# Linear-attention layer of a four-layer trunk: value projection in two parts, later affine on ScalarE, longer rows of convolution matrices

## The chip, the cores and the metric

The kernel runs on one core of a Trainium2 chip, in float32. The metric is the device time of one execution in microseconds (us), as the median of several runs.

## The reference

The input x is [1, 512, 64, 64]. Four layers follow each other, each of the form `x = x + layer(groupnorm(x))`: an attention with distances (layer 0), two gated convolution layers (1 and 2), and the linear attention with a depthwise 5x5 convolution that is changed here (layer 3). Cut to what matters:

```python
def _L3_conv_ref(x, ...):                       # D = 256, EPS = 1e-5
    qkv0 = affine(conv1x1(x, w_qkv), s_qkv, b_qkv)            # 768 channels
    agg = affine(depthwise5x5(qkv0, w_dw), s_dw, b_dw)
    agg = agg * (w_pw * s_pw) + b_pw
    q, k, v = split(concat([qkv0, agg], axis=1), 3)           # 512 channels each
    q = relu(q) + EPS
    k = relu(k) + EPS
    z = einsum('bc,bcn->bn', k.mean(axis=2), q) + EPS
    vk = einsum('bcn,bdn->bcd', v * N ** -0.5, k * N ** -0.5)
    attn = einsum('bcd,bdn->bcn', vk, q) / z
    y = attn * g_norm + bt_norm + v
    return affine(conv1x1(y, w_proj), s_proj, b_proj)

x = x + L0(gn(x));  x = x + L1(gn(x));  x = x + L2(gn(x));  x = x + L3(gn(x))
```

In chunks of 128 channels, qkv0 has chunks 0 to 5 and agg chunks 0 to 5. So q is qkv0[0..3], k is qkv0[4..5] with agg[0..1], and v is agg[2..5]. The projection of v, `w_proj v`, does not depend on the attention and can be added to x by itself.

## The kernel before

The state X, 512 channels by 4096 pixels, stays in SBUF as four chunks of 128 partitions through all layers. Pixels are held as 4 x 8 planes (by the pixel's row and column modulo), and a block is 512 pixels. In layer 3 a block has the indices `hf` (0 or 1, half of the image) and `q` (0 to 3).

**Instruction order.** The program is written with a framework that plans the order: on each engine a planner places instructions by their written order and by when its cost model believes them ready, and it adds the semaphore waits. Only TensorE keeps the written order (`keep_in_program_order`, L684 and L1335). Each engine then executes its list in order; DMAs are issued from the lists of SyncE (SP), ScalarE and POOL, so an issue that waits holds up what stands behind it there.

**Layer 3, making qkv0.** `fused` and `group` make qkv0 (with products saved by sums and differences, `_Seven`), and `put` writes each result through a plane tile to a DRAM buffer G (L711). The pieces are kept in the list `made`, 81 of them, and `fill(n)` executes the next n. The weights come from `weights` (L1112), which loads a chunk and multiplies it on POOL by a broadcast row of `s_qkv`; `scales` (L1122) loads that row into buffers of the pool `kv`, in two loads on ScalarE's queue.

**The depthwise convolution.** `_PlaneConv.conv` handles chunk i, half hf as block-structured matrix products. `load` (L716) brings two rounds at once: the matrices T (one DMA, L720) and two copies of the input S (two DMAs, L737), of which ScalarE (L744) or VectorE (L742) makes the shifted second copies. A convolution is two halves of 64 products (128 matmul instructions each). After each half VectorE transposes the two PSUM banks into `turned` (L798), after the second it makes four blocks `agg` (L807), and the callback `finish` is called for each: in layer 3 `affine` (L1291), an activation on ScalarE. `conv` yields after the first half and at its end. `ahead` issues the loads of the next convolution early; `sp3` has four buffers each of T and S.

**`convs(units, between)`** (L1299) runs convolutions one after the other, and at each yield it takes one function of `between`, TensorE work that goes between two halves. In the list of before, the order is (0,0), (1,0) with four fills, then (2,0), (0,1), (3,0), (4,0), (5,0) with four fills for the first four yields and then `added` (a bias row, 16 tiny products), `prepare(0,0)` (loads and sums k) and three `turned` (transposes of k, L1345).

**The steps.** For each of the eight blocks, `step(t)` (L1359), four times, transposes k and v (L1336, evicted as kT on ScalarE and vT on VectorE), projects v for output chunk t (`part`, L1348: four products with `w_proj`, an eviction `pv` on ScalarE, an addition to X on POOL, L1355), and accumulates the four v-k products in the banks `vkp`. The steps of hf=0 run among the convolutions (1,1) to (5,1), the steps of hf=1 after them. All products, convolution halves and transposes share four PSUM banks, `ps_mm`. Then q is loaded, and the output is made block by block.

Of the kernel before, what the change touches and what calls it, by code (L numbers as in the profile page):

```python
# [25 lines left out]
D = C // HEADS  # L26
GROUP = 16
GN_EPS = 1e-5


KS = 7
# [93 lines left out]
@with_exitstack  # L125
def trunk_kernel(ctx: ExitStack, tc: tile.TileContext, a: dict, out: bass.AP):
    nc = tc.nc

    base = ctx.enter_context(tc.tile_pool(name="base", bufs=1))
    small = ctx.enter_context(tc.tile_pool(name="small", bufs=1))  # L130


    X = base.tile([P, NC, N], FP, tag="X", name="X")
    for b in range(NB):
        for c in range(NC):
            eng = nc.sync if c % 2 == 0 else nc.scalar
# [28 lines left out]

    neg2 = base.tile([D, 1], FP, tag="neg2", name="neg2")
    nc.vector.memset(neg2, -2.0)

    def new_stats():
        return small.tile([P, NC, NB, 6], FP, tag="stats", name="stats")  # L170

    centered = _Centered(tc, small)

    dram = ctx.enter_context(tc.tile_pool(name="dram", bufs=1, space=bass.MemoryType.DRAM))
    F = [dram.tile([P, FORM.planes, FORM.plane], FP, tag=f"F{i}", name=f"F{i}") for i in range(NDW)]
    F3 = [
        dram.tile([P, FORM3.planes, FORM3.plane], FP, tag=f"G{i}", name=f"G{i}")
        for i in range(NQKV)
    ]
    Z = dram.tile([NB, BLK], FP, tag="Z", name="Z")  # L180

    stats = _attention(tc, a, X, ident, gmask, neg2, small, new_stats, centered)
    stats = _gated_convs(tc, a, X, vcol, gmask, small, new_stats, centered, stats, F)
    _linear_attention(tc, a, X, vcol, vall, ident, gmask, small, centered, stats, F3, Z, out)


def _attention_general(tc, a, X, O, ident, neg2):
# [469 lines left out]
class _PlaneConv:  # L657
# [58 lines left out]
    def load(self, i, hf, wT, r):  # L716
        nc, f = self.nc, self.f
        nl = self.nl
        w = self.sp3.tile([P, nl, 4, f.by * f.bx, 32], FP, tag="T", name="T")
        nc.sync.dma_start(  # L720
            out=w.rearrange("p r g b m -> p r (g b m)"),
            in_=wT[i, r : r + nl].rearrange("r p x -> p r x"),
        )
        run = (f.part + f.by - 1 + (f.jy - 1) * f.by) * f.fw
        S = self.sp3.tile([P, nl, 4, run], FP, tag="S", name="S")
        F = self.F[i]
        chan = f.planes * f.plane
# [174 lines left out]
def _gated_convs(ctx, tc, a, X, vcol, gmask, small, new_stats, centered, stats, F):  # L902
# [7 lines left out]
    hp = ctx.enter_context(tc.tile_pool(name="ch", bufs=5))  # L910
    ps_mm = ctx.enter_context(tc.tile_pool(name="ps_mm", bufs=4, space=PSUM))
    ps_cv = ctx.enter_context(tc.tile_pool(name="ps_cv", bufs=4, space=PSUM))
    pc = _PlaneConv(ctx, tc, FORM, F, ps_cv, 2, 4, False)

    for layer in ("L1", "L2"):
        pre = f"{layer}_conv_"
# [133 lines left out]


@with_exitstack
def _linear_attention(ctx, tc, a, X, vcol, vall, ident, gmask, small, centered, stats, F, Z, out):

# [48 lines left out]
    with ExitStack() as st:  # L1103
        wp = st.enter_context(tc.tile_pool(name="lw", bufs=1))
        w2p = st.enter_context(tc.tile_pool(name="lw2", bufs=4))
        tmp = st.enter_context(tc.tile_pool(name="ltmp", bufs=5))
        kvp = st.enter_context(tc.tile_pool(name="kv", bufs=34))
        ps_vk = st.enter_context(tc.tile_pool(name="ps_vk", bufs=1, space=PSUM))
        ps_mm = st.enter_context(tc.tile_pool(name="ps_mm", bufs=4, space=PSUM))
        pc = _PlaneConv(st, tc, f, F, ps_mm, 2, 4, True)  # L1110

        def weights(i, scale):  # L1112
            t = w2p.tile([P, NROW], FP, tag="w", name="w_qkv")[:, 0:C].rearrange(
                "p (c n) -> p c n", c=NC
            )
            nc.sync.dma_start(out=t, in_=a["L3_w_qkv"][i])
            nc.gpsimd.tensor_tensor(
                t, t, scale.unsqueeze(1).to_broadcast([P, NC, P]), ALU.mult
            )
            return t  # L1120

        def scales(i, n):  # L1122

            t = kvp.tile([P, BLK], FP, tag="kv", name="s_qkv")[:, 0 : n * P]
            nc.scalar.dma_start(
                out=t, in_=bass.AP(a["L3_s"].tensor, a["L3_s"].offset + i * P, [[0, P], [1, n * P]])
            )
            return t.rearrange("p (i m) -> p i m", m=P)

        s_qkv = scales(0, 4)  # L1130
        w_qkv = [weights(i, s_qkv[:, i]) for i in range(4)]

        alpha = wp.tile([P, NQKV], FP, tag="alpha", name="alpha")
        beta = wp.tile([P, NQKV], FP, tag="beta", name="beta")
# [120 lines left out]
            return [lambda: taken(2 * k), lambda: taken(2 * k + 1)]  # L1255

        def more_weights():
            s4 = scales(4, 2)
            for i in (4, 5):
                w_qkv.append(centered.scaled(weights(i, s4[:, i - 4]), rstd, nc.scalar))  # L1260

        dve, pool = nc.vector, nc.gpsimd
        made = [
# [24 lines left out]
        def conv(i, hf, primed):  # L1288
            agg[i, hf] = [kvp.tile([P, BLK], FP, tag="kv", name=f"agg{i}") for _ in range(4)]

            def affine(t):  # L1291
                nc.scalar.activation(  # L1292
                    t, t, AF.Relu if i < 2 else AF.Identity,
                    bias=beta[:, i : i + 1], scale=alpha[:, i : i + 1],
                )

            return pc.conv(i, hf, a["L3_T"], affine, agg[i, hf], primed)

        def convs(units, between, before=0):  # L1299


            between = list(between)
            if before:
                pc.ahead(*units[0], a["L3_T"])
                for _ in range(before):
                    between.pop(0)()
            for n, u in enumerate(units):
                for part, _ in enumerate(conv(*u, n + before > 0)):
                    if between:
                        between.pop(0)()  # L1310
                    if part == 0 and n + 1 < len(units):
                        pc.ahead(*units[n + 1], a["L3_T"])
            for f in between:
                f()

        agg = {}
        def gather(hf, q):
# [27 lines left out]
            def turned(t):  # L1345
                ahead[t] = turn(ks, t, "kT", kvp, "kv")

            def part(o, v):  # L1348
                ps = product(lambda c: w_proj[:, c, ts(o, P)], v)
                t = tmp.tile([P, BLK], FP, tag="tmp", name="pv")  # L1350
                nc.scalar.activation(
                    t, ps, AF.Identity, bias=pbias[:, o : o + 1], scale=vcol(pre + "s_proj", o)
                )
                xs = blocks(X[:, o, :])[:, hf, q]
                nc.gpsimd.tensor_tensor(  # L1355
                    xs, xs, t.rearrange("p (x n) -> p x n", x=XW), ALU.add
                )

            def step(t):  # L1359
                v = [agg[2 + i, hf][q] for i in range(NC)]  # L1360
                kT = ahead.pop(t) if t in ahead else turn(ks, t, "kT")
                vT = turn(v, t, "vT")
                part(t, v)
                for c in range(NC):
                    pc.matmul(
                        vkp[c],
# [3 lines left out]
                        stop=(b == NB - 1 and t == QT - 1),  # L1370
                    )

            return prepare, turned, [lambda t=t: step(t) for t in range(QT)]

        def both(*pieces):
            return lambda: [f() for f in pieces]
# [26 lines left out]
        def prepare(hf, q):  # L1403
            return blks[hf, q][0]
# [4 lines left out]
        def steps(hf, q):  # L1409
            return list(blks[hf, q][2])  # L1410

        convs(
            [(2, 0), (0, 1), (3, 0), (4, 0), (5, 0)],
            fills(6, 6, 6, 6)
            + [added, prepare(0, 0), turned(0, 0, 0), turned(0, 0, 1), turned(0, 0, 2)],
        )
        vkp = [ps_vk.tile([P, C], FP, tag=f"vk{c}", name=f"vkp{c}") for c in range(NC)]
        for q in range(3):
# [196 lines left out]
```

## Time and profile before

| | |
|---|---|
| time, median of 3 runs | 3947.94 us (3947.69 to 3948.85) |
| the profiled execution's own time | 3946.93 us |
| its span, from first to last instruction | 3945.0 us |
| TensorE (PE) busy | 3856.6 us, 98% |
| VectorE (DVE) busy | 2363.8 us, 60% |
| ScalarE (ACT) busy | 1968.2 us, 50% |
| POOL busy | 96.2 us, 2% |
| mean granted TensorE clock | 0.991 |
| T loads: layers 1 and 2 / layer 3 | 112 x 384 KB / 48 x 256 KB |

Busy shares are means over four quite different layers. The granted clock is the share of full speed at which TensorE was allowed to run; a product at half clock counts as busy for twice the time. The last layer begins at about 3306 us, and the steps of hf=1 end at about 3808 us. In the profile's lines an arrow reads "written from read"; in brackets stands the idle time before, and what ended it.

### The profile page before, as it was taken

How to read it: one execution, taken by the hardware profiler on the slowest of the kernel's cores; microseconds unless marked ns; L12 is line 12 of the kernel's file. 1: busy time of each engine (PE TensorE's matmuls, PEld its weight loads, DVE VectorE, ACT ScalarE, POOL GpSimd, SP SyncE). 2: the span in 40 equal slices, each digit the busy share in tenths (PEclk: the TensorE clock that was granted, in tenths of full speed). 3: DMA queues.
4: the chain of work that ended last, by engine and by line, in shares of the span. 5: the costliest groups of instructions: out<-in, count | busy, mean ns of one | idle time of the engine just before them, and what ended most of it. 6: DMA issues, size and time to landing. Idle time of an engine off the chain costs nothing. (4 is left out here: it accounts for less than half of the span.)

```text
span 3945.0 us, 81422 instructions
## 1 busy us (share of the span) xinstructions
PE 3856.6 (98%) x35622; PEld 1721.0 (44%) x35622; DVE 2363.8 (60%) x2607; ACT 1968.2 (50%) x2841; POOL 96.2 (2%) x84
## 2 busy tenths in 40 slices
PE   6999999999999999999999989999999998989999
PEld 4533345333354333453333345554455543455544
DVE  3677763777737777547767633466434567664435
ACT  3577753777726777446656544451344522343210
POOL 0000000000000000000000000000000000201110
PEclk9999999999999999999999999999999999989999
DMA  2000000000000000000000045651255521563334
GB/s 97 9 1 1 1 1 9 1 1 1 1 1 9 1 1 1 1 9 1 1 1 1 1 130 154 186 154 57 69 161 177 162 56 51 153 171 85 92 90 142
DMA packets 214631, 221.52 MB, mean 56 GB/s; under 512 B 13416, under 2 KB 179688, under 8 KB 214144
## 3 DMA queue, kind: packets, MB, share of 16 engines
q1 hardware_dynamic: 187312, 157.12, 14.6%
q10 hardware_dynamic: 26928, 59.11, 4.1%
q8 instruction: 281, 4.60, 0.5%
q14 instruction: 78, 0.64, 0.1%
q0 software_dynamic: 32, 0.06, 0.0%
HBM read 156.46 MB, written 59.77 MB: 55 GB/s over the span
## 5 line engine op out<-in xcount | busy, mean ns | idle before, releaser
L507 ACT ACTIVATE pt<-ps_s,A 128x512 f32<-128x512 f32 x2048 | 1286.3, 687 | 554.8 <-PE ps_s L499 527.0
L590 DVE TENSOR_TENSOR acc<-acc,pt 128x1024 f32<-128x1024 f32 x960 | 1175.4, 1224 | 331.8 <-ACT pt L507 306.0
L517 PE MATMUL av<-pt,V 64*64 64x512 f32 x8192 | 1112.5, 590 | 0.9 <-ACT pt L507 0.9
L499 PE MATMUL ps_s<-O,K 64*64 64x512 f32 x8192 | 1111.5, 589 | 0.0
L517 PEld LDWEIGHTS av<-pt,V 64*64 64x64 f32 x8192 | 339.7, 133 | 557.2 <-issue 525.4
L499 PEld LDWEIGHTS ps_s<-O,K 64*64 64x64 f32 x8192 | 334.3, 133 | 553.7 <-issue 308.6
L744 ACT COPY S<-S 32x1295 f32<-32x1295 f32 (+1 forms) x272 | 341.0, 1256 | 300.6 <-DMA S<-F 203.4
L684 PE MATMUL ps<-X,w_in_L 128*128 128x512 f32 x896 | 405.9, 605 | 5.4 <-DVE w_in_L L357 5.4
L957 DVE TENSOR_SCALAR plane<-ps,vec 128x512 f32<-128x512 f32 x112 | 83.8, 748 | 295.3 <-PE ps L684 252.3
L684 PEld LDWEIGHTS ps<-X,w_in_L 128*128 128x128 f32 x896 | 167.0, 192 | 205.1 <-issue 195.4
L684 PE MATMUL ps_cv<-S,T 64*32 64x128 f32 x13824 | 240.5, 278 | 13.3 <-issue 5.5
L684 PEld LDWEIGHTS ps_cv<-S,T 64*32 64x32 f32 x13824 | 199.1, 107 | 117.7 <-issue 81.6
L454 PE MATMUL ps_qk<-X,wqkv 128*128 128x512 f32 x512 | 227.2, 597 | 2.8 <-ACT wqkv L354 2.8
L684 PE MATMUL ps<-h,w_out_L 128*128 128x512 f32 x512 | 228.4, 599 | 0.5 <-DVE X L991 0.5
L346 ACT ACTIVATE X<-X,gn_less 128x512 f32<-128x512 f32 x120 | 77.1, 710 | 217.5 <-DVE gn_less L100 206.4
L458 ACT ACTIVATE O<-ps_qk 128x512 f32<-128x512 f32 x32 | 19.1, 596 | 258.3 <-PE ps_qk L454 258.3
L1016 ACT ACTIVATE h<-h,vec 128x1024 f32<-128x1024 f32 x56 | 63.7, 1148 | 167.3 <-DVE h L804 167.1
L684 PEld LDWEIGHTS ps<-h,w_out_L 128*128 128x128 f32 x512 | 94.3, 190 | 116.6 <-issue 100.5
L454 PEld LDWEIGHTS ps_qk<-X,wqkv 128*128 128x128 f32 x512 | 95.5, 192 | 113.5 <-issue 109.9
L979 DVE SCALAR_TENSOR_TENSOR h<-ps,vec,h 128x512 f32<-128x512 f32 x112 | 82.5, 743 | 103.1 <-PE ps L684 99.0
L684 PE MATMUL ps<-h,pw_L 128*128 128x512 f32 x320 | 142.6, 598 | 0.7 <-DVE X L995 0.7
L460 DVE TENSOR_SCALAR K<-ps_qk 128x512 f32<-128x512 f32 x32 | 22.1, 692 | 187.0 <-PE ps_qk L454 187.0
(153 smaller groups left out, 2745.5 us busy)
## 6 DMA issues: line engine op xcount, KB each, us to landing
T<-in_L_T_dram SPq DMA_DIRECT2D x112, 384.0 KB, 4.0
F<-plane ACTq DMA_DIRECT2D x112, 324.0 KB, 2.7
S<-F SPq DMA_DIRECT2D x224, 162.0 KB, 4.1
row<-G SPq DMA_DIRECT2D x80, 272.0 KB, 3.7
S<-G SPq DMA_DIRECT2D x96, 153.0 KB, 4.5
G<-plane ACTq DMA_DIRECT2D x48, 289.0 KB, 2.3
T<-in_L_T_dram SPq DMA_DIRECT2D x48, 256.0 KB, 4.1
out_dram<-y SPq DMA_DIRECT2D x32, 256.0 KB, 2.0
```

The source lines that it names most:

```text
L346: self.nc.scalar.activation(xs, xs, AF.Identity, bias=less)
L454: nc.tensor.matmul(ps, w[:, n, c, :], X[:, c, cols], start=(c == 0), stop=(c == NC - 1))
L460: nc.vector.tensor_scalar(K[:, cols], ps, gain_in, None, ALU.mult)
L499: nc.tensor.matmul(ps[ts(half, D), ts(h, BLK)], K[rows, t * P + half * D : t * P + (half + 1) * D], QO[pair][rows, cols], start=True, stop ...
L507: nc.scalar.activation(pt[:, ts(h, BLK)], ps[:, ts(h, BLK)], AF.Exp, bias=A[:, t, h : h + 1])
L517: nc.tensor.matmul(av[half][rows, :], V[keys, t, rows], pt[keys, ts(h, BLK)], start=(t == 0), stop=(t == NT - 1),)
L590: nc.vector.tensor_add(acc, acc, pt)
L684: self.tc.keep_in_program_order(self.nc.tensor.matmul(*args, **kw))
L744: nc.scalar.copy(second, first)
L957: lambda dst, src: nc.vector.tensor_scalar(dst, src, vcol(pre + "b_in", 1 + i), None, ALU.add),
L979: nc.vector.scalar_tensor_tensor(d, ps, bias, d, ALU.add, ALU.mult)
L1016: nc.scalar.activation(t, t, AF.Identity, bias=vcol(pre + "dw_b", i))
```

## The change

Five edits, four of them in layer 3.

1. `part(o, c0, c1)` projects only the chunks c0 to c1 of v. For the blocks of hf=0 the chunks 0 and 1 (agg[2], agg[3]) are projected in 16 early parts, each with its own eviction (without bias) and its own addition to X; the steps of hf=0 project chunks 2 and 3. The steps of hf=1 project all four as before.
2. The convolutions are run in another order: (2,0), (3,0) with the four fills, then (0,1), (4,0), (5,0) with `added`, the 16 early parts (1, 3, 3, 3, 3, 3) and `prepare(0,0)` between their halves. The three early `turned` of block (0,0) are gone; its steps do those transposes. (0,1) is now the first of its list, so its loads are written at its start and not in the previous convolution.
3. `affine` is put into a list `late`, and run after the next piece of `between`.
4. `s_qkv` is loaded once, from POOL's queue before layers 1 and 2, into a pool of its own; the pool `kv` has 33 buffers in place of 34.
5. The matrices T are laid out in DRAM so that the two rounds of a load are contiguous for each partition: one row of twice the length per partition. This holds for layers 1 to 3.

```diff
+    late = ctx.enter_context(tc.tile_pool(name="late", bufs=1))
+    s_qkv = late.tile([P, NQKV, P], FP, tag="s_qkv", name="s_qkv")
+    nc.gpsimd.dma_start(
+        out=s_qkv.rearrange("p i m -> p (i m)"),
+        in_=bass.AP(a["L3_s"].tensor, a["L3_s"].offset, [[0, P], [1, NQKV * P]]),
+    )
     stats = _gated_convs(tc, a, X, vcol, gmask, small, new_stats, centered, stats, F)
...
         nc.sync.dma_start(
-            out=w.rearrange("p r g b m -> p r (g b m)"),
-            in_=wT[i, r : r + nl].rearrange("r p x -> p r x"),
+            out=w.rearrange("p r g b m -> p (r g b m)"), in_=wT[i, r // nl],
         )
...
-        kvp = st.enter_context(tc.tile_pool(name="kv", bufs=34))
+        kvp = st.enter_context(tc.tile_pool(name="kv", bufs=33))
...
-        s_qkv = scales(0, 4)
-        w_qkv = [weights(i, s_qkv[:, i]) for i in range(4)]
+        w_qkv = [weights(i) for i in range(4)]
...
             def affine(t):
-                nc.scalar.activation(
-                    t, t, AF.Relu if i < 2 else AF.Identity,
-                    bias=beta[:, i : i + 1], scale=alpha[:, i : i + 1],
+                late.append(
+                    lambda: nc.scalar.activation(
+                        t, t, AF.Relu if i < 2 else AF.Identity,
+                        bias=beta[:, i : i + 1], scale=alpha[:, i : i + 1],
+                    )
                 )
...
                     if between:
                         between.pop(0)()
+                    while late:
+                        late.pop(0)()
                     if part == 0 and n + 1 < len(units):
                         pc.ahead(*units[n + 1], a["L3_T"])
...
-            def part(o, v):
-                ps = product(lambda c: w_proj[:, c, ts(o, P)], v)
+            def part(o, c0, c1):
+
+                ps = product(
+                    lambda c: w_proj[:, c0 + c, ts(o, P)],
+                    [agg[2 + c, hf][q] for c in range(c0, c1)],
+                )
                 t = tmp.tile([P, BLK], FP, tag="tmp", name="pv")
-                nc.scalar.activation(
-                    t, ps, AF.Identity, bias=pbias[:, o : o + 1], scale=vcol(pre + "s_proj", o)
-                )
+                scale = vcol(pre + "s_proj", o)
+                if c1 == NC:
+                    nc.scalar.activation(t, ps, AF.Identity, bias=pbias[:, o : o + 1], scale=scale)
+                else:
+                    nc.scalar.activation(t, ps, AF.Copy, scale=scale)
...
-                part(t, v)
+                part(t, 0 if hf else 2, NC)
...
+            early = [lambda o=o: part(o, 0, 2) for o in range(NC)]
+            return prepare, turned, [lambda t=t: step(t) for t in range(QT)], early
...
+        convs([(2, 0), (3, 0)], fills(6, 6, 6, 6))
+
+        early = [f for q in range(4) for f in blks[0, q][3]]
         convs(
-            [(2, 0), (0, 1), (3, 0), (4, 0), (5, 0)],
-            fills(6, 6, 6, 6)
-            + [added, prepare(0, 0), turned(0, 0, 0), turned(0, 0, 1), turned(0, 0, 2)],
+            [(0, 1), (4, 0), (5, 0)],
+            [
+                both(added, *early[:1]),
+                both(*early[1:4]),
+                both(*early[4:7]),
+                both(*early[7:10], prepare(0, 0)),
+                both(*early[10:13]),
+                both(*early[13:]),
+            ],
         )
...
-        return T.reshape(n // P, f.nr, P, -1)
+        T = T.reshape(n // P, f.nr // NL, NL, P, -1)
+        return T.swapaxes(2, 3).reshape(n // P, f.nr // NL, P, -1)
```

More of the change, by code (lines that the diff above doesn't have):

```diff
@@ L28 @@
 GN_EPS = 1e-5
+NL = 2
 KS = 7
@@ L182, in trunk_kernel @@
     stats = _attention(tc, a, X, ident, gmask, neg2, small, new_stats, centered)
+    late = ctx.enter_context(tc.tile_pool(name="late", bufs=1))
[4 more added lines that the diff above has]
+    )
     stats = _gated_convs(tc, a, X, vcol, gmask, small, new_stats, centered, stats, F)
-    _linear_attention(tc, a, X, vcol, vall, ident, gmask, small, centered, stats, F3, Z, out)
+    _linear_attention(tc, a, X, vcol, vall, ident, gmask, small, centered, stats, F3, Z, s_qkv, out)
 def _attention_general(tc, a, X, O, ident, neg2):
@@ L912, in _gated_convs @@
     ps_cv = ctx.enter_context(tc.tile_pool(name="ps_cv", bufs=4, space=PSUM))
-    pc = _PlaneConv(ctx, tc, FORM, F, ps_cv, 2, 4, False)
+    pc = _PlaneConv(ctx, tc, FORM, F, ps_cv, NL, 4, False)
     for layer in ("L1", "L2"):
@@ L1052, in _linear_attention @@
 @with_exitstack
-def _linear_attention(ctx, tc, a, X, vcol, vall, ident, gmask, small, centered, stats, F, Z, out):
+def _linear_attention(ctx, tc, a, X, vcol, vall, ident, gmask, small, centered, stats, F, Z, s_qkv, out):
     nc = tc.nc
@@ L1106, in _linear_attention, with weights @@
         tmp = st.enter_context(tc.tile_pool(name="ltmp", bufs=5))
-        kvp = st.enter_context(tc.tile_pool(name="kv", bufs=34))
+        kvp = st.enter_context(tc.tile_pool(name="kv", bufs=33))
         ps_vk = st.enter_context(tc.tile_pool(name="ps_vk", bufs=1, space=PSUM))
         ps_mm = st.enter_context(tc.tile_pool(name="ps_mm", bufs=4, space=PSUM))
-        pc = _PlaneConv(st, tc, f, F, ps_mm, 2, 4, True)
-        def weights(i, scale):
+        pc = _PlaneConv(st, tc, f, F, ps_mm, NL, 4, True)
+        def weights(i):
             t = w2p.tile([P, NROW], FP, tag="w", name="w_qkv")[:, 0:C].rearrange(
@@ L1117, in weights @@
             nc.gpsimd.tensor_tensor(
-                t, t, scale.unsqueeze(1).to_broadcast([P, NC, P]), ALU.mult
+                t, t, s_qkv[:, i].unsqueeze(1).to_broadcast([P, NC, P]), ALU.mult
             )
             return t
[L1122 to L1126, printed above, removed]
-            )
-            return t.rearrange("p (i m) -> p i m", m=P)
-        s_qkv = scales(0, 4)
-        w_qkv = [weights(i, s_qkv[:, i]) for i in range(4)]
+        w_qkv = [weights(i) for i in range(4)]
         alpha = wp.tile([P, NQKV], FP, tag="alpha", name="alpha")
@@ L1257, in more_weights @@
         def more_weights():
-            s4 = scales(4, 2)
             for i in (4, 5):
-                w_qkv.append(centered.scaled(weights(i, s4[:, i - 4]), rstd, nc.scalar))
+                w_qkv.append(centered.scaled(weights(i), rstd, nc.scalar))
         dve, pool = nc.vector, nc.gpsimd
@@ L1291, in affine @@
             def affine(t):
-                nc.scalar.activation(
-                    t, t, AF.Relu if i < 2 else AF.Identity,
-                    bias=beta[:, i : i + 1], scale=alpha[:, i : i + 1],
+                late.append(
[3 more added lines that the diff above has]
+                    )
                 )
             return pc.conv(i, hf, a["L3_T"], affine, agg[i, hf], primed)
+        late = []
         def convs(units, between, before=0):
@@ L1346, in turned @@
                 ahead[t] = turn(ks, t, "kT", kvp, "kv")
-            def part(o, v):
-                ps = product(lambda c: w_proj[:, c, ts(o, P)], v)
-                t = tmp.tile([P, BLK], FP, tag="tmp", name="pv")
-                nc.scalar.activation(
-                    t, ps, AF.Identity, bias=pbias[:, o : o + 1], scale=vcol(pre + "s_proj", o)
-                )
+            def part(o, c0, c1):
[3 more added lines that the diff above has]
+                )
+                t = tmp.tile([P, BLK], FP, tag="tmp", name="pv")
+                scale = vcol(pre + "s_proj", o)
[3 more added lines that the diff above has]
+                    nc.scalar.activation(t, ps, AF.Copy, scale=scale)
                 xs = blocks(X[:, o, :])[:, hf, q]
@@ L1371, in step @@
                     )
-            return prepare, turned, [lambda t=t: step(t) for t in range(QT)]
+            early = [lambda o=o: part(o, 0, 2) for o in range(NC)]
+            return prepare, turned, [lambda t=t: step(t) for t in range(QT)], early
         def both(*pieces):
```

## The prediction

> **What bounds the kernel now.** I read the page's slices first. TensorE is 98% busy over the whole span, so only the places where it is not busy can be worth anything: at most 3945.0 - 3856.6 = 88 us, plus what it loses where it is busy at a reduced clock. In the last layer (from 3306 us on) two slices have a PE digit of 8 and one a clock digit of 8. I cut that stretch into pieces with the view of busy time by windows (columns: window, its length, then busy us of PE, PEld, DVE, ACT, POOL with instruction counts, granted clock, DMA share, GB/s):
>
> ```profile
> 3490.00:3500.00 10.00, 10.00 (x170) 6.98 (x169) 5.83 (x10) 2.93 (x4) 0.00 (x0) 1.00 0.51 158
> 3505.00:3510.00 5.00, 3.05 (x83) 1.68 (x66) 4.78 (x6) 2.48 (x3) 0.00 (x0) 0.50 1.10 238
> 3510.00:3515.00 5.00, 3.56 (x68) 2.37 (x68) 4.91 (x11) 3.33 (x5) 0.00 (x0) 0.50 0.73 158
> 3520.00:3525.00 5.00, 1.93 (x56) 1.46 (x56) 4.91 (x6) 2.73 (x4) 0.00 (x0) 0.64 0.69 163
> 3525.00:3530.00 5.00, 3.68 (x76) 2.51 (x76) 2.56 (x4) 4.31 (x6) 0.00 (x0) 0.50 0.55 144
> 3540.00:3545.00 5.00, 5.00 (x78) 2.47 (x80) 3.20 (x8) 3.89 (x4) 1.92 (x1) 1.00 0.00 0
> ```
>
> From 3500 to 3537 TensorE works 40 to 80% of the time, mostly at half clock, while VectorE is close to full in several pieces. This is the run of convolutions (3,0), (4,0), (5,0), which has almost no other TensorE work between. The chain of waits says what it runs through:
>
> ```profile
> 3495.17 5.13 DMA G<-plane
> ...
> 3501.77 3.32 PE ps_cv L684 x112
> ...
> 3505.12 1.33 DVE turned L798 x2
> ...
> 3506.54 3.81 DVE agg L807 x4
> ...
> 3511.44 1.93 PE ps_cv L684 x56
> ...
> 3518.56 1.33 DVE turned L798 x2
> ...
> 3537.25 3.44 PE ps L684 x8
> 3540.68 3.43 PE vkp L684 x8
> ```
>
> A convolution half is followed by transposes on VectorE (`turned`, `agg`), then copies of S, then the next half. The chain leaves TensorE only in that stretch; after 3537 it is TensorE from step to step. A second, smaller hole is in the timeline (start, length, engine, what; in brackets the idle time before and what ended it):
>
> ```profile
> 3402.28 3.51 ACT L1292 ACTIVATE agg<-agg,beta,alpha 128x512 f32<-128x512 f32 x4 [7.84 <-DVE agg L807]
> 3404.80 0.80 DVE L1176 SCALAR_TENSOR_TENSOR plane<-ps,step_b,kept 128x256 f32<-128x256 f32 x2
> 3406.74 3.78 PE L684 MATMUL ps<-X,w_qkv 128*128 128x512 f32 x4 [4.50 <-ACT kept L1226]
> 3541.70 1.92 POOL L1355 TENSOR_TENSOR X<-X,pv 128x512 f32<-128x512 f32 x1 [79.47 <-ACT pv L1351]
> ```
>
> ScalarE stood in `affine` (waiting for VectorE's transposes) while TensorE needed the eviction `kept` behind it: 4.5 us idle, and the clock falls to 0.53 in 3405 to 3410. The last line is the row of one POOL addition (most of the 32 take 1.27 us), used below.
>
> **The change, part by part.**
>
> *Value products by parts.* Each `part` of hf=0 had four products; two of them (chunks 2, 3 of v, here 0 and 1 of `agg[2..3]`) now run earlier. Four products are 3.44 us (the x8 row above: each product appears as two instructions), so two are 1.72 us. Sixteen early parts: 16 x 1.72 = 27.5 us of TensorE moved from the steps, where TensorE is the bound, into the hole. The later steps lose the same 27.5 us.
>
> What the hole holds now: from 3494.5 (end of the last `fill`) to 3537.1 (start of the first `part`) 42.6 us. TensorE's own work there at full clock: six convolution halves x 1.97 (rows "ps_cv x128" of 1.96 to 1.97 us elsewhere in the chain) = 11.8, `added` 3.7, four groups of transposes x 0.44 = 1.8; together 17.3. So 25.3 us are lost.
>
> Afterwards, same place with (0,1), (4,0), (5,0): halves 11.8, `added` 3.7, early parts 27.5, and the two transposes of the first step 0.9: 43.9 us of TensorE. Its rivals for the bound: VectorE per convolution 4 x 0.66 (`turned`) + 4 x 0.96 (`agg`) + 4 x 0.78 (S) = 9.5, three of them 28.6, plus `prepare` (4 k at 0.32, 4 ksum at 0.63) and `pbias` 4.3: 33 us. ScalarE per convolution 4 x 1.20 (S) + 4 x 0.81 (`affine`) = 8.0, three of them 24, plus 16 new evictions x 0.78 (the row of `pv`) = 12.5: 36.6 us. POOL 16 new additions x 1.27 = 20.3 us. DMA: 8 loads of S (153 KB) and 4 of T (256 KB) per convolution, 2.2 MB in 14 us, 160 GB/s, where 238 was moved above. TensorE is the largest, by 7 us, and each part-yield puts 5.2 us of products next to a 2 us half, so the transposes and copies have something beside them. If it never waited, the first `part` would start at 3494.5 + 43.9 = 3538.4, 1.3 us later than now.
>
> It will wait somewhat. At the start VectorE stands in the last `put` for the plane's DMA (the 5.13 us above) and holds the banks of the first half; the tiny products of `added` do not keep the clock (0.59 in 3500 to 3505). I take 3 us for that. ScalarE is 83% used and in order, with `affine` and S copies between evictions that free the four banks of `ps_mm`: 3 us. Bounds: 0, and 12 if each of six halves waits 2 us. So the first `part` starts about 7.3 us later than now.
>
> *A rule against it.* The POOL additions run beside VectorE's copies of S. In the trace these 48 copies have a median of 0.78 us and a longest of 1.87, the long ones beside POOL. The Trainium skill, "SBUF — State Buffer", section "SBUF: two separate sides", says that a GpSimd instruction and a two-port VectorE instruction exclude each other for the whole instruction, so 12 copies here could each wait for an addition: 12 x 1.1 = 13 us, VectorE 46 us, and it would pass TensorE by 2 to 3 us. By the row, half of them hit for 0.6 us each, 3 to 4 us, VectorE stays under 37. I take the row: nothing on the path; the 3 us go into the range.
>
> *Turned transposes.* Three `turned` calls of (0,0) are gone from the hole and are back in steps 0 to 2 of (0,0): the first is counted above, two more are 2 x 0.44 = +0.9 us on the path.
>
> *Later steps with less cover.* A step of hf=0 was 0.87 + 3.44 + 3.43 us and becomes 6.0. The vT copy (0.69 on VectorE) had 3.44 us of products to hide under and now 1.72. Where `agg` (3.8 us) and `prepare` (about 4 us) stand ahead of it on VectorE, TensorE and through it the vkp products wait; before, one such wait cost 0.99 us at 3568, and around 3662 to 3673 the chain already ran 11.8 us through VectorE with TensorE just covered. I take 1 us for each of four blocks: +4 (bounds 0 and 10).
>
> *`affine` later.* `late` puts the 48 `affine` behind the next filler on ScalarE, four at a time. At 3402 the eviction would go first. The next hold is then the bank that the put of 3404.80, behind VectorE's transposes, frees at 3405.6: about 1.6 us of wait in place of 4.5, and no loss of clock (2.8 us, from about 5.6 us at half). Gain 2.9 + 2.8 = 5.7; I take -5.5. Bounds: 0 if the planner keeps its order on ScalarE (it does reorder: on VectorE the put of L1176 ran ahead of an earlier-written L1173), 7.3 if all of it goes. What is queued behind a late `affine`: S copies, and the ksum of the same chunk; both have a filler of 5 us or more.
>
> *s_qkv through POOL's queue.* Two DMAs leave the ScalarE queue at the layer's start; one of 384 KB goes to POOL's at the start of the convolution layers. At 3314.1 POOL waited for s_qkv (6.8 us to landing) with w_qkv landing within about 0.7 us of it, so -0.7. At 2293 the new transfer shares the DMA with w_in, which VectorE awaited at 2299.65 by 0.31 us: 384 KB at 370 GB/s is up to +1.0; POOL's issue itself is ahead of an X update with 3 us to spare. Bounds -1.5 and +1; I take -0.2. One kv buffer fewer: the count where diff, w_sum and agg meet is 34, but two sets overlap only until the third fill, before the last agg is written; 0, covered by that fill, and about 2 us if not.
>
> *Longer rows of T.* 160 loads with half as many rows, twice as long. L1 and L2 are TensorE-bound (50.00 and 49.69 of 50 us busy in the windows at 3000 and 3050), so 0 there whatever a load costs. In the hole the chain met one load per convolution; a 256 KB load of w_in lands in 2.8 us against T's 4.1, so at most 1.3 x 3 = 4 us, which the early products cover anyway: 0. The other end is +1 if the planner, which knows the new sizes, shifts something.
>
> *Sum:* hole +7.3, steps -27.5 + 0.9 + 4, `affine` -5.5, s_qkv -0.2: -21.0 us. On the profiled execution's own time, 3946.93 (span 3945.0 and 1.9 around it), that gives 3925.9; the median of the runs is 1.0 above it, so 3927.
>
> **The rivals.**
>
> *Partly filled* (2 in 10): ScalarE's order binds in the hole and the holes of the later steps are larger. With 12 us of holds in the hole and 10 in the steps: +13.3 - 27.5 + 0.9 + 10 - 5.5 = -9: 3939. For it: ScalarE 83% and VectorE up to 85% used. Against: they were never this starved of a third party's work.
>
> *Displaced* (1 in 10, with most of its times no change): TensorE executes in written order, so if each half waits for copies that come only after the products before it, the 27.5 us extend the hole one for one: hole 70 us, steps -27.5, sum about 0 to -6: 3945. Against: in the hole TensorE waits for VectorE, which the products do not use.
>
> *Slower, the clock* (6 in 100): the gate stays at half through the hole because every half ends in a short wait. 43.9 us of work become 88; against the 42.6 of now that is +45, less 27.5, and +4: 3948 + 17 = 3965 with `affine` bringing -5. It decides from about 27 us of full-clock work done at half. For it: 81% busy in 3515 to 3520 still had 0.70. Against: 2.92 of 5 us busy at 3440 had 1.00, and the products come in runs of 5.2 us.
>
> **How the numbers follow.** About 0.2% (8 us) is what a measurement of this kernel can tell from no change. Forecast 0.64, partly filled 0.2, displaced 0.1, clock 0.06. Faster takes the first two: 0.84; same 0.10; slower 0.06. Range: the forecast with its bounds runs from 3914 (no holds in the hole, 0 in the steps, -7 from `affine`) to 3936; it is drawn out to 3941 to take in the partly filled case.
>
> **What would show it.** Right: PE digits 9 and clock 1.0 from about 3505 to 3540; "ps<-agg,w_proj" with 32 products among the convolutions; steps of 6.0 us; the 4.5 us wait for `kept` gone; POOL busy about 96 + 20 us. Wrong: clock 0.5 to 0.7 still there with the products in it; waits PE <- DVE vT of over 5 us in the steps; "ps_cv <- ACT S" growing; the wait for s_qkv gone but a longer one at 2300.

## The result, and the profile after

The changed kernel takes 3932.01 us (median of 6 runs, 3927.94 to 3933.80), against 3948.39 us for the kernel before in the same series (6 runs, 3946.99 to 3950.05). The ratio is 0.9957, with a 95% interval of 0.9944 to 0.9970: a gain of 16.4 us by the medians, and of 0.43% by the ratio. The profiled execution of after took 3927.94 us (span 3926.1), the lowest of its six. Against the profiled execution of before the gain is 19.0 us, so 2.6 us of it is which run was profiled.

First the page's slices of after (busy tenths in 40 equal slices; only the lines of TensorE, VectorE and clock), with the busy line above them:

```profile
span 3926.1 us, 81449 instructions
...
PE 3847.3 (98%) x35622; PEld 1714.3 (44%) x35622; DVE 2370.2 (60%) x2607; ACT 1976.8 (50%) x2857; POOL 119.3 (3%) x101
...
PE   6999999999999999999999989999999999999999
...
DVE  3577763777736777637767733466534576675435
...
PEclk9999999999999999999999999999999999999999
```

The two slices of the last layer that had a PE digit of 8, and the clock digit of 8, are gone. POOL has 23.1 us more than before (96.2): 16 more additions, at 1.27 us each 20.3, and 0.6 for issuing the load of `s_qkv`. VectorE has 6.4 us more, although the change gives it nothing to do; that comes back below.

Next the view of busy time by windows of after, over the same run of convolutions (window, length, then busy us of PE, PEld, DVE, ACT, POOL with instruction counts, granted clock, DMA share, GB/s):

```profile
3490.00:3500.00 10.00, 10.00 (x246) 7.78 (x235) 3.73 (x9) 2.07 (x3) 1.33 (x1) 0.83 0.78 210
3500.00:3510.00 10.00, 10.00 (x187) 5.38 (x172) 9.24 (x12) 7.14 (x10) 3.84 (x4) 1.00 0.61 163
3510.00:3520.00 10.00, 10.00 (x147) 5.01 (x146) 9.84 (x11) 7.10 (x9) 6.24 (x5) 1.00 0.66 172
3520.00:3530.00 10.00, 10.00 (x271) 5.75 (x269) 9.15 (x14) 9.32 (x12) 5.67 (x4) 1.00 0.50 134
3530.00:3540.00 10.00, 8.42 (x40) 3.81 (x24) 9.80 (x13) 7.21 (x11) 6.01 (x5) 1.00 0.70 176
3540.00:3550.00 10.00, 8.15 (x148) 4.91 (x149) 4.37 (x8) 2.39 (x3) 1.27 (x1) 1.00 0.39 101
3650.00:3660.00 10.00, 7.82 (x267) 6.11 (x265) 6.54 (x12) 5.69 (x8) 1.33 (x1) 0.83 0.22 60
```

From 3490 to 3538 TensorE is full, at a clock of 1.0 apart from one stretch near 3497. Read the DVE column too: from 3500 to 3540 it is 9.2 to 9.8 of 10. VectorE is as near its limit there as TensorE, and TensorE's first wait comes at the end, in the windows from 3530 on. The chain of waits of after through this stretch (start, length, what):

```profile
3491.49 3.66 PE ps_pb L693 x32
3495.16 2.71 PE ps L693 x4
3497.87 2.71 PE ps_cv L693 x128
3500.58 5.35 PE ps L693 x12
3505.92 2.01 PE ps_cv L693 x123
...
3530.22 5.35 PE ps L693 x12
3535.57 0.89 PE ps_t L1341 x8
...
3539.17 0.67 ACT kT L1345
...
3541.85 3.67 PE vkp L693 x8
```

Groups of three early parts (5.35 us) alternate with convolution halves (2.0 us), as forecast. The first part and the first half behind `added` take 2.71 us each instead of 1.72 and 1.97: they ran partly at half clock. At the end there is a hold before the first `vkp` products. The waits of TensorE from 3535 to 3670 in after (us in total, times, longest):

```profile
PE vkp L693 <- ACT S L752: 3.2, 1, 3.2
PE ps_cv L693 <- DVE turned L806: 2.2, 2, 2.0
PE vkp L693 <- DVE vT L1347: 1.4, 2, 1.2
PE vkp L693 <- ACT kT L1345: 1.4, 1, 1.4
...
```

And the timeline of after at the small hole among the fills, and at the end of the large one (in brackets the idle time before and what ended it):

```profile
3398.29 2.61 ACT L1291 ACTIVATE agg<-agg,beta,alpha 128x512 f32<-128x512 f32 x3 [8.04 <-DVE agg L815]
3400.81 0.67 ACT L1225 ACTIVATE kept<-ps,vec 128x512 f32<-128x512 f32 x1
3401.53 3.78 PE L693 MATMUL ps<-X,w_qkv 128*128 128x512 f32 x4 [3.31 <-ACT kept L1225]
...
3537.12 2.89 DVE L1102 TENSOR_SCALAR k<-row 128x256 f32<-128x256 f32 x3
3539.85 1.26 DVE L1335 TENSOR_REDUCE ksum<-k 128x1 f32<-128x512 f32 x2
3541.02 0.69 DVE L1347 COPY vT<-ps_t 128x512 f32<-128x512 f32 x1
3541.85 3.67 PE L693 MATMUL vkp<-kT,vT 128*128 128x512 f32 x8 [3.24 <-ACT S L752]
```

The wait for `kept` is 3.31 us, not gone: three `affine` still stand ahead of it (the x3 row). At 3541.85 the releaser named is a copy of S, which these products do not read. They read kT, done at 3539.84, and vT, done at 3541.71 behind `prepare`'s k and ksum on VectorE. The S copy only ended at about the same moment (3541.73).

Where the 19.0 us between the two profiled executions come from, cut at the same instructions in both timelines (us):

| stretch | before | after | difference |
|---|---|---|---|
| start to first product of layer 1 | 2300.4 | 2301.1 | +0.6 |
| layers 1 and 2 | 1005.9 | 1004.2 | -1.7 |
| from there to the first product of layer 3 | 11.0 | 9.0 | -2.0 |
| to the end of the last `fill` | 177.2 | 175.3 | -1.9 |
| to the first product of the steps | 42.6 | 47.2 | +4.6 |
| to the last `vkp` product | 270.4 | 252.6 | -17.8 |
| to the end | 137.6 | 136.8 | -0.8 |

### The profile page after: what moved, and what is told of

It reads as the page before. It is cut to its first block, busy times and chain, and to the rows that moved or that the text cites. A ratio compares the mean times of both kernels' runs of the same rounds, so it can differ in the third digit from the quotient of the medians.

```text
span 3926.1 us, 81449 instructions
## 1 busy us (share of the span) xinstructions
PE 3847.3 (98%) x35622; PEld 1714.3 (44%) x35622; DVE 2370.2 (60%) x2607; ACT 1976.8 (50%) x2857; POOL 119.3 (3%) x101
## 5 line engine op out<-in xcount | busy, mean ns | idle before, releaser
L693 PE MATMUL ps_cv<-S,T 64*32 64x128 f32 x13824 | 231.5, 273 | 4.8 <-DVE turned L806 2.2
```

The costliest lines, as they stand in the source:

```text
L693: self.tc.keep_in_program_order(self.nc.tensor.matmul(*args, **kw))
```

## The experiments

The `only_...` kernels are before with one part of the change. The others are after with one edit. The time of before beside each is that of runs on the same chip.

**The split alone.** Before with the new `part`, the early parts and the new order; the other edits left out.

```diff
+        convs([(2, 0), (3, 0)], fills(6, 6, 6, 6))
+        early = [f for q in range(4) for f in blks[0, q][3]]
         convs(
-            [(2, 0), (0, 1), (3, 0), (4, 0), (5, 0)],
+            [(0, 1), (4, 0), (5, 0)],
...
-                part(t, v)
+                part(t, 0 if hf else 2, NC)
```

> Before, with the split value projection and the new convolution order alone (affine at once, s_qkv late, short rows of T). Theory (the split carries the change): -13 to -16 us against before (hole +6 to the first vkp product, steps -19.5): ratio 0.9960 to 0.9968; the 4.5 us wait for kept at about 3402 and the 11.0 us gap at the layer's start are both still there. Rival (the split only moves work, the rest brought the gain): within 4 us of before.

Measured: 3932.67 us against 3947.42, ratio 0.9965 (0.9952 to 0.9979). These are 14.8 of the whole change's 16.4 us, and the two intervals overlap. In its timeline the wait for `kept` is 4.5 us and the gap before layer 3 is 11.0, as before: the split does not touch them, and carries nearly the whole gain without them. Its waits from 3490 to 3670 begin with another engine than after's:

```profile
PE ps L684 <- ACT pv L1359: 3.2, 2, 2.4
...
```

Here TensorE waits for evictions `pv` on ScalarE, and its first `vkp` products do not wait.

**Longer rows of T alone.**

```diff
-            out=w.rearrange("p r g b m -> p r (g b m)"),
-            in_=wT[i, r : r + nl].rearrange("r p x -> p r x"),
+            out=w.rearrange("p r g b m -> p (r g b m)"), in_=wT[i, r // nl],
```

> Before, with the longer rows of T alone. Theory: no change, within 2 us (1.000 +- 0.0005), TensorE covers the loads; DMA packets fall by 20480. Rival (the loads are on the chain in the hole, and their shorter time also helps layers 1 and 2, which ended 1.7 us sooner after their start in the changed kernel): -2 to -4 us, layers 1 and 2 shorter by about 1.7 us in this profile too.

Measured: 3946.65 us, ratio 0.9998 (0.9990 to 1.0006). Nothing, although the time to landing of the loads in layer 3 goes from 4.1 to 3.8 us.

**s_qkv alone.**

```diff
-        s_qkv = scales(0, 4)
-        w_qkv = [weights(i, s_qkv[:, i]) for i in range(4)]
+        w_qkv = [weights(i) for i in range(4)]
...
+    nc.gpsimd.dma_start(
+        out=s_qkv.rearrange("p i m -> p (i m)"),
```

> Before, with s_qkv loaded once by POOL ahead of layers 1 and 2 (kv 33) alone. Theory: the gap from layer 2's last product to layer 3's first goes from 11.0 to about 9.0 us, as in the changed kernel, and layer 1's start is not later by more than 0.5 us: -2 us, -0.0005. Rival (the new transfer delays w_in by as much): the gap shorter, layer 1's first product later by 1 to 2 us, sum 0.

Measured: 3946.83 us, ratio 1.0002 (0.9994 to 1.0010): inconclusive in the time. In the timeline the gap before the first product of layer 3 is 9.5 us. It is 8.9 to 9.6 in every kernel that holds this edit, and 11.0 in the three that do not. So 1.4 to 2.1 us of the gap are gone, less than this time can show.

**`affine` at once.** After without the list `late`.

```diff
-                late.append(
-                    lambda: nc.scalar.activation(
-                        t, t, AF.Relu if i < 2 else AF.Identity,
+                nc.scalar.activation(
+                    t, t, AF.Relu if i < 2 else AF.Identity,
```

> The changed kernel with affine written at once, as before. Theory (the planner put three affine ahead of kept in both, so late changed the order little): within 2 us of the changed kernel, i.e. about -15 us against before, wait for kept 3 to 4.5 us. Rival (late is worth the 5.5 us of the prediction, the rest of the change less): -10 us against before, and the wait for kept at 4.5 us with ScalarE held behind four affine.

Measured: 3929.00 us, ratio 0.9954 (0.9941 to 0.9968), no slower than after. The wait for `kept` is 4.5 us here and 3.3 in after. On ScalarE, before and this kernel have four `affine` ahead of `kept`, and after has three: writing them later moved one. In this kernel too TensorE waits for `pv` (3.1 us, 2.3 of it at the end of the stretch), and the first `vkp` products do not wait.

**No early parts.** After with all four products in the steps again, and the new order kept.

```diff
-                part(t, 0 if hf else 2, NC)
+                part(t, 0, NC)
...
+            [added, both(), both(), prepare(0, 0), both(), both()],
```

> The changed kernel without the 16 early parts: the new convolution order and the rest stay, the steps of hf=0 project all four chunks again. Theory (the products in the hole are the gain): the hole starves again, with granted clock 0.5 to 0.7 between the convolutions, hole to the first vkp product 44 to 49 us in place of 52.4, steps longer by 17 to 20 us: within 3 us of before less the 2 us of s_qkv. Rival (the new convolution order, by which (4,0) no longer waits for the plane DMA, brings the gain by itself): -8 us or more against before.

Measured: 3942.57 us, ratio 0.9988 (0.9981 to 0.9995), so 12 of after's 16 us are gone (0.9988 against 0.9957). Its stretch from the last `fill` to the first `vkp` product is 46.6 us (46.0 before, 52.4 after), and two stretches of 17.1 and 13.7 us at half clock are back in it.

**One chunk early.** Early parts with one product instead of two; the steps do three.

```diff
-                part(t, 0 if hf else 2, NC)
+                part(t, 0 if hf else 1, NC)
...
-            early = [lambda o=o: part(o, 0, 2) for o in range(NC)]
+            early = [lambda o=o: part(o, 0, 1) for o in range(NC)]
```

> The changed kernel with one chunk of v projected early in place of two; the steps of hf=0 project three. Theory: 13.8 us of products move instead of 27.5. The hole then has 30 us of TensorE work against about 36 us of ScalarE and VectorE work, so it is bound by those: hole 44 to 48 us, granted clock below 1 in parts of it; steps 13.8 us less than before minus smaller waits (cover 2.6 us): sum -9 to -13 us against before. Rival (with two chunks the lost cover in the steps eats up the second chunk's gain): as fast as the changed kernel or faster.

Measured: 3946.56 us, ratio 0.9997 (0.9989 to 1.0006): the gain is gone altogether. The stretch to the first `vkp` product, expected at 44 to 48 us, is 55.4, longer than after's 52.4, with 13.8 us less TensorE work in it at full clock. The chain of waits of this kernel, in the middle of it:

```profile
3518.87 1.32 DVE turned L806 x2
...
3521.41 1.36 DVE S L750
...
3522.80 2.95 DVE agg L815 x3
...
3528.60 1.93 PE ps_cv L693 x56
```

And its busy time by windows there:

```profile
3523.00:3533.00 10.00, 5.92 (x123) 3.46 (x118) 8.24 (x14) 5.20 (x6) 2.14 (x2) 0.71 0.36 93
```

The chain is VectorE's again, TensorE is 59% busy, and the clock is 0.71. The 16 evictions and the 16 additions are the same as with two products, while TensorE has half as much to do beside them. So the length of this stretch is not set by TensorE's products alone.

**No additions for the early parts.** This kernel leaves out the 16 additions of the early parts to X, and computes all else.

```diff
+                if c1 == NC:
-                nc.gpsimd.tensor_tensor(
+                  nc.gpsimd.tensor_tensor(
                     xs, xs, t.rearrange(
```

> The changed kernel without the POOL additions of the 16 early parts (so the early half of hf=0's value projection is missing from the output). Theory (the hole is bound by VectorE as much as by TensorE, and POOL's additions lengthen VectorE's copies and k): S copies in the hole back to 0.78 us each, VectorE busy there 4 to 6 us less, the first vkp product's wait falls from 3.2 us to below 1.5: -2 to -3 us against the changed kernel. Rival (POOL and VectorE don't get in each other's way, TensorE alone bounds the hole): no change, wait 3 us.

Measured: 3926.89 us, ratio 0.9952 (0.9938 to 0.9965). This interval overlaps with after's, so the times do not tell the two apart. Nor can the 5.1 us between the two profiled executions be put down to the additions: 3.1 of them lie in the fills, ahead of the first early part (the last section shows why). What the additions do is read inside the stretch. The copies of S and the k on VectorE, in the views of one tile (min, median and max in ns), first of after and then of this kernel:

```profile
L750 DVE COPY S<-S x12: 781/892/1886, 3498.2 to 3541.7; 32x1207 f32<-32x1207 f32 x12
L1102 DVE TENSOR_SCALAR k<-row x8: 369/422/1451, 3521.5 to 3539.6; 128x256 f32<-128x256 f32 x8
```

```profile
L750 DVE COPY S<-S x12: 772/781/782, 3495.2 to 3536.9; 32x1207 f32<-32x1207 f32 x12
L1102 DVE TENSOR_SCALAR k<-row x8: 368/396/414, 3518.6 to 3534.8; 128x256 f32<-128x256 f32 x8
```

And the sums from the last `fill` to the first `vkp` product by windows, of after and of this kernel:

```profile
3489.46:3541.85 52.39, 48.97 (x877) 28.30 (x877) 44.03 (x59) 34.55 (x42) 24.35 (x17) 0.97 0.66 174
```

```profile
3485.83:3537.03 51.20, 48.99 (x876) 27.96 (x876) 37.48 (x59) 32.82 (x41) 0.00 (x0) 0.97 0.71 175
```

With POOL idle (24.35 to 0.00 us), no copy takes longer than 782 ns and no k longer than 414, and VectorE is busy 6.55 us less with the same 59 instructions: 3.44 of it in the copies, 3.12 in k. The wait before the first `vkp` products falls from 3.24 to 1.27 us, and the stretch from 52.4 to 51.2. So POOL's additions slow VectorE. How, the timeline of after shows:

```profile
3503.29 1.27 POOL L1366 TENSOR_TENSOR X<-X,pv 128x512 f32<-128x512 f32 x1 [3.20 <-ACT pv L1364]
...
3504.03 1.19 DVE L750 COPY S<-S 32x1207 f32<-32x1207 f32 x1
```

The copy began while the addition ran, and ended some 0.65 us after it. So do all six long copies of the stretch (0.64 to 0.65 us after), and the three long k (0.27 to 0.30 us after). Copies that began first took their usual 0.78 us, and the additions beside two of them took 1.42 and 1.86. The other work of VectorE there (`turned`, `agg`, ksum) takes as long beside POOL as without it, within 0.2 us in each sum. This agrees with the Trainium skill, "SBUF — State Buffer", section "SBUF: two separate sides": of a GpSimd instruction and a VectorE instruction in a two-port mode, whichever starts first holds the shared ports for its whole instruction.

**One chunk without additions.** Both edits: 16 early parts of one product each, their additions left out.

> One chunk projected early, without the POOL additions of the early parts (so that part is missing from the output). Theory (with one chunk the hole is a chain of VectorE transposes, S copies and short products, and the copies stretched by POOL are in it): hole from 55.4 to about 50 us, S copies in it 0.78 us: -5 us against the one-chunk kernel. Rival (the 16 extra evictions on ScalarE and the four shared banks make the chain): hole stays at 54 to 56 us.

Measured: 3939.84 us, ratio 0.9982 (0.9975 to 0.9989), 6.7 us below one chunk with additions. In the profiled executions the stretch shrinks from 55.4 to 51.8 us; another 3.6 us lie in the fills, as in the last experiment. That is still as long as the 51.2 of two products without additions, and 5 us longer than with no early parts. So the additions are one part of what the early parts cost there. What the other 5 us are (ScalarE's evictions, the four shared banks, the order of the copies) no run tells apart.

**The bias row moved into the fills.** `added` runs between fills, where other products surround it.

```diff
-        fill(4)
+        fill(1)
+        added()
+        fill(3)
...
-                both(added, *early[:1]),
+                both(*early[:1]),
```

> The changed kernel with the bias row's 16 tiny products moved out of the hole to between the fills before (1,0) ends. Theory (VectorE is late at the end of the hole anyway): the hole to the first vkp product shortens by less than 3 us though TensorE has 3.7 us less to do there and no half-clock stretch of 3.4 us; the fills grow by 3.7 us: 0 to +3 us. Rival (TensorE and its clock bound the hole): hole 5.4 us shorter, fills 3.7 longer: -1.7 us.

Measured: 3936.34 us, ratio 0.9972 (0.9961 to 0.9982), some 4 us slower than after by the medians, though the intervals overlap. Taking 3.7 us of TensorE work out of the stretch shortens it by 1.4 us only (52.4 to 51.0), and the fills grow by 7.2 (175.3 to 182.5), with two stretches of half clock that were not there. One of them, at 3437.73, stands right behind `added`, and the one at the start of the stretch is gone: it went with `added`. The wait before the first `vkp` products is 3.7 us: VectorE is late there, not TensorE.

**`affine` tied behind `kept`.** The same list, with an ordering edge on ScalarE that the planner must keep.

```diff
-            nc.scalar.activation(t, ps, AF.Identity, bias=bias)
+            kept.append(nc.scalar.activation(t, ps, AF.Identity, bias=bias))
...
+                    if late and made:
+                        with tc.issue_after(kept[-1].ins):
+                            while late:
+                                late.pop(0)()
```

> The changed kernel with affine in the first four convolutions tied behind the last kept on ScalarE, so that the planner cannot put it ahead. Theory (late failed because the planner kept affine ahead of kept): the wait of 3.3 to 4.5 us at about 3402 falls to 1.7 us or less (then the bank freed by VectorE's put), the half-clock stretch of 6.8 us behind it goes: -4 us against the changed kernel. Rival (the bank is what holds, kept only named for it): the wait stays at 3 us, same time as the changed kernel.

Measured: 3929.26 us, ratio 0.9954 (0.9940 to 0.9967). In its waits (TensorE, 3306 to 3490):

```profile
PE ps L693 <- ACT kept L1225: 1.5, 1, 1.5
```

That is the 1.6 us that the prediction expected. The 6.8 us of half clock behind the hole are gone too (3.4 us at 3436 are new), and the fills take 173.0 us in place of 175.3. Those 2.3 us are within the spread of the runs, so the time neither shows nor excludes them.

**`prepare` written behind the step.** In the steps, k and ksum of the next block are written after vT.

```diff
-            convs([(q + 1, 1)], [s[0], both(prepare(0, q + 1), s[1])] + s[2:], 1)
+            convs([(q + 1, 1)], [s[0], both(s[1], prepare(0, q + 1))] + s[2:], 1)
```

> The changed kernel with prepare of the next block written after the step it shares a yield with, not before. Theory (the 3.2 us wait of the first vkp product is for vT, which stands behind prepare's k and ksum on VectorE): that wait falls below 1.5 us, the sum of TensorE's idle time in the steps of hf=0 falls from 8.7 us to 4 to 6: -2 to -4 us. Rival (kT behind affine and pv on ScalarE, as the trace names it): the wait stays, no change.

Measured: 3932.50 us, ratio 0.9961 (0.9948 to 0.9975). The edit did nothing: on VectorE, k and ksum are still ahead of vT, and the wait is 3.0 us. As with `late`, the planner placed them where its own costs say. This run decides nothing about the theory.

**Both ties.** `affine` behind `kept`, and `prepare` behind vT on VectorE, both by ordering edges.

```diff
-                    nc.vector.tensor_copy(sb, ps)
+                    vts.append(nc.vector.tensor_copy(sb, ps))
...
+        def behind(f):
+            def run():
+                with tc.issue_after(vts[-1].ins):
+                    f()
+            return run
...
-            convs([(q + 1, 1)], [s[0], both(prepare(0, q + 1), s[1])] + s[2:], 1)
+            convs([(q + 1, 1)], [s[0], both(behind(prepare(0, q + 1)), s[1])] + s[2:], 1)
```

> The changed kernel with affine tied behind kept in the first convolutions, and prepare of the next block tied behind the vT copy of the step before on VectorE. Theory (the first vkp product waits for vT, which prepare's k and ksum delay): that wait falls from 3.1 us to about 1.3 us, then kT behind affine and pv on ScalarE holds it; sum of TensorE's idle time in the steps of hf=0 falls by 2 to 3 us; with the wait for kept at 1.5 us, -4 to -6 us against the changed kernel. Rival (kT on ScalarE is the last for it all along): wait stays at 3 us, time as with affine tied alone.

Measured: 3922.72 us (5 runs, 3918.03 to 3924.10), ratio 0.9936 (0.9922 to 0.9949): 25 us below before. Against after it is 8 us by the ratios, with intervals that just overlap, and 5.2 us by the profiled executions: 2.9 in the fills and 3.6 from the last `fill` to the last `vkp` product, with small differences elsewhere. The timeline of this kernel at the end of the stretch (its L1353 is after's L1347):

```profile
3537.23 0.69 DVE L1353 COPY vT<-ps_t 128x512 f32<-128x512 f32 x1 [0.36 <-PE ps_t L1347]
3537.96 2.17 DVE L1102 TENSOR_SCALAR k<-row 128x256 f32<-128x256 f32 x4
3538.83 0.67 ACT L1351 ACTIVATE kT<-ps_t,eps 128x512 f32<-128x512 f32 x1
...
3539.56 3.70 PE L693 MATMUL vkp<-kT,vT 128*128 128x512 f32 x8 [0.71 <-ACT kT L1351]
```

vT is now ahead of k, and 0.71 us remain of the 3.24, for kT on ScalarE. The waits of TensorE from 3530 to 3670 in this kernel:

```profile
PE ps_cv L693 <- DVE turned L806: 2.2, 2, 2.1
PE vkp L693 <- DVE vT L1353: 1.2, 1, 1.2
PE vkp L693 <- ACT kT L1351: 0.7, 1, 0.7
```

The `vkp` products wait 1.9 us in place of after's 6.0, and from the first `vkp` product to the last convolution half it takes 114.4 us in place of 118.2.

## Why the prediction was right or wrong

**The direction and the cause were right.** The forecast sum was -21.0 us. The profiled pair gave -19.0, the medians -16.4; the forecast of 3927 lies 5 us below the measured 3932. That the split does it is shown from both ends: alone it gives nine tenths of the gain, and without the early parts only a quarter of it is left. None of the rivals occurred as described. Displaced, partly filled and the clock all have TensorE idle or at half in the stretch, and it is full there up to the hold at its end.

That the sum came within 2 us is in part luck. The steps and `affine` together gained 8.4 us less than forecast. Against that stand 2.7 us that the stretch cost less, 1.8 us more from s_qkv, and 1.9 us in the rest of the table, which the change does not explain.

**The stretch between the fills and the steps** was put at +7.3 us to the first product of the steps, and is +4.6. The 3 us for `added` at reduced clock were about 1.7, by the 2.71 us rows against 1.72 and 1.97. The 3 us for ScalarE's order did not appear in after before the steps began (0.2 us for `pv`). They did in the kernels with the split alone and with `affine` at once (3.2 and 3.1 us): which engine TensorE waits for at the end of the stretch depends on the planner's order.

**The steps** were put at -22.6 (-27.5, +0.9, +4) and gave -17.8. The term that was mis-sized is the lost cover, +4. The holds are 3.24, 1.23, 0.37, 1.37 and 2.01 us, 8.2 in all, against 0.99 and 0.45 before: +6.8. The mechanism named (vT behind other work on VectorE) makes two of them, 3.24 and 1.23. The 1.37 for kT on ScalarE and the 0.37 and 2.01 for the banks that `turned` frees were not named. One stretch of half clock behind the last of them (a half in 3.9 us where 2.0 is usual) adds 1.8. That is +8.6 in place of +4, and closes the sum within 0.2 us. The kernel with both ties confirms the mechanism of the largest: with vT ahead, it falls by 2.5 us.

**The rule against it.** The prediction took the row (half of the copies hit for 0.6 us, 3 to 4 us in all, VectorE under 37) over the skill's rule at its worst (13 us, VectorE 46). For the copies the row was right: six of twelve were stretched, by 3.4 us together. The rule could be read in before as well: its six long copies all began during an instruction of POOL, and ended 0.64 to 0.65 us after it. Yet VectorE came to 44.0 us, near the rule's figure, because the sum lacked two other terms. The conflict also hit k (3.1 us), which was not reckoned. And VectorE has 37.5 us of work there without any conflict, not 33: the planner put k and ksum of a second block into the stretch, so 8 and 8 instructions run there where the sum had 4 and 4. "Nothing on the path" was the wrong step. In after two of the stretched k stand ahead of the first vT (2.0 us more than usual), and without the additions the wait is 2.0 us shorter and the stretch 1.2.

**`affine` later** was put at -5.5 and failed. The lower end, "0 if the planner keeps its order on ScalarE", is nearly what happened: one of four `affine` moved, 1.2 us of wait went, the half clock stayed, and the time without the edit is no worse. With the order forced, the wait is 1.5, where 1.6 was forecast. So the cause of the hole was read rightly, and the edit as written does not remove it.

**s_qkv** was put at -0.2, and its gap shrank by 2.0. POOL's wait in front of the first scaling went from 3.18 to 1.18 us, with w_qkv as the one that it now waits for. That w_qkv itself lands sooner without the other load beside it is argued, not shown.

**The rows of T** at 0 are borne out: 0.9998. The -1.7 us in layers 1 and 2 are no effect of the change. There the kernels differ by up to 2.9 us (1003.5 to 1006.4), without relation to the edits.

## What to carry to other kernels

When idle TensorE time is filled with work from elsewhere, look at what the work left behind was covering, and at the second engine of the stretch: here VectorE was at 92 to 98% as soon as TensorE was full, and the longest of the further waits ended on it. Where a planner orders the engines, writing a step later in the program is a wish; read the engine's list in the trace, and use an explicit edge where the order matters (the same two ideas gave no time that could be measured when rewritten, and some 8 us together when tied). Additions on POOL are not free because POOL is idle: price them by what VectorE loses, in each of its instructions that can stand beside them.

## What the runs showed of the hardware

Half clock comes in pieces. In every profiled execution the stretches at reduced clock inside layer 3 are 3.4, 6.8, 10.2, 13.7, 17.1 or 20.5 us, multiples of 3.4 us, which fits the window of about 3.4 us in the Trainium skill, "TensorE: Matmul & The Clock Gate", Part 1. Within one execution they also begin on one grid of 3.41 us.

The price of a hold depends on where it falls on this grid. A wait of 3.3 us for `kept` stands in seven of the traces; in five it was followed by 6.8 us at half clock, in two (the ones without additions) by none. Here are after and the kernel without additions, cut at their grids:

```profile
3396.97:3400.38 3.41, 1.25 (x3) 0.19 (x1) 3.38 (x5) 1.92 (x3) 0.10 (x1) 1.00 0.70 169
3400.38:3407.21 6.83, 5.68 (x7) 2.52 (x8) 5.82 (x12) 5.52 (x7) 0.00 (x0) 0.50 0.17 63
```

```profile
3395.83:3399.25 3.42, 1.57 (x4) 0.38 (x2) 3.39 (x5) 1.63 (x2) 0.42 (x1) 1.00 0.74 170
3399.25:3406.08 6.83, 5.37 (x134) 3.18 (x136) 6.74 (x14) 5.86 (x7) 0.00 (x0) 1.00 0.22 85
```

In after the wait left TensorE busy for 37% of one grid step (1.25 of 3.41 us), and half clock followed; in the other kernel for 46% in the emptiest step, and none did. The same holds throughout: over all 14 traces, from 3320 to 3800 us and at full clock, each of the 28 steps with TensorE busy for up to 40% was followed by half clock, and none of those with more than 48%, apart from the step of `added` (below); between 41 and 48%, 8 of 14 were. So the fills are 3.1 us shorter without the additions mainly because of where the wait fell on the grid, which the edit does not set in any way that a run shows. A piece of 3.4 us at half clock does 1.7 us less work, so a hold's price moves in such steps, which may be why the same kernel spreads over 6 us from run to run; no run isolated that.

A run of tiny products can bring half clock too. The 16 products of `added` keep TensorE busy for 3.7 us, and yet in all 14 traces a stretch at half clock begins at their end (from 0.1 us before to 1.0 us after), also where they were moved into the fills.

POOL and VectorE slow each other: in 52 us, 16 additions cost twelve copies and eight k of VectorE 6.55 us, and single copies went from 0.78 to 1.89 us. The additions grew too, from 1.27 us each to 1.45 on average (23.3 us for the 16).
